# A two-layer transformer block on one core: the dense stream is written in even portions, with the next tokens' norm and gates moved

## The chip, the core and the metric

The kernel runs on one core of a Trainium2 chip. Its time is the device time in microseconds (us) of one execution; the median of three runs is compared. The engines are TensorE (PE; PEld is its weight load), VectorE (DVE), ScalarE (ACT), GpSimd (POOL) and SyncE (SP), which here only issues DMAs.

## The reference

The input is 4 sequences of 1024 tokens with 256 channels, float32. Two layers follow each other, each an attention part and a feed-forward part with adaptive layer norms (a norm, then a scale and a shift for each sequence, and a gate on the way back to the residual). Only the second layer is touched here:

```python
h = _layernorm(x) * (1 + ca) + sa
x = x + ga * _L1_attn_ref(h, ...)
h = _layernorm(x) * (1 + cb) + sb
x = x + gb * _L1_ffn_ref(h, ...)

def _L1_attn_ref(X, ...):                     # for each pair of tokens i, j of a sequence
    q, k = X @ Wq.T, X @ Wk.T                 # 64 channels
    e = relu(signed_sqrt(q[:, :, None, :] + k[:, None, :, :]))
    scores = e @ Wphi
    ex = exp(scores - max(scores))
    part1, Ew = ex @ Vy, einsum('bij,bija->bia', ex, e)
    return (part1 + Ew @ We_w.T + We_b * denom) / denom

def _L1_ffn_ref(x, ...):                      # 256 -> 1024 -> 1024 -> 1024 -> 256
    h = silu(x @ w1.T * s1) * (x @ w2.T * s2)
    h = gelu(h @ h1.T * sh1)
    h = gelu(h @ h2.T * sh2)
    return h @ w3.T * s3
```

## The kernel before

Up to about 1110 us the first layer runs. Then `pair_attention` does the second layer's attention and, woven into it, three other things.

**The attention loop.** The 4096 queries are taken in 128 blocks of 32. A block has 8 *turns*. In a turn VectorE weighs two tiles of 128 x 1024 (`weigh`, L1478: a product with a sum), and pairs for blocks ahead are made (`begin`, `make`): GpSimd or ScalarE or VectorE adds the query and clamps (L1402, L1407, L1427, L1416), ScalarE takes the square root (L1428), TensorE forms the scores (L1432). A ring of 14 tiles lets the making run ahead of the weighing. At turn p == 5 the scores' maximum is taken (`top`, L1442), at p == 6 the exponential (`exps`, L1451). ScalarE's tables for square root and exponential are changed there and back in each block (ACT_TABLE_LOAD). After every fourth block a task, `finish`, puts 128 tokens' attention together.

**The dense stream.** The feed-forward part is done for groups of 256 tokens, 16 groups in all. A group is put in the queue `stream` when `finish` has done its second 128 tokens, so every 8 blocks. It is a generator, `dense(j)`: `head` loads the residual and norms it; `gate` forms the first product, w1 (four pieces, L1263, evicted at L1255); silu; the second product, w2 (`up`, L1263, evicted with the product at L1298); two hidden layers of 1024 x 1024 (L1333, evicted at L1317), each followed by gelu; the output product (L1354), the gate (L1364) and the residual's sum (L1365). Two tiles, `wide[0]` and `wide[1]`, hold all that lies between. Weights come in tiles of 512 KB in a pool of four (`weights`, L1047), on SP's queue.

Ahead of the groups the stream has `first_rest` (the rest of the first layer) and, for each further sequence, `prepare` (its keys, queries and values; it uses `wide` too).

**The order.** All is written in one fixed order on the host; each engine then follows its own instructions in order. After the weighing of a turn `work(room)` advances first the tasks and then the stream:

```python
ROOM = (4, 6, 6, 6, 6, 4, 3, 6)      # units of TensorE's work in the turns of a block
...
got = next(of[0], self_done)         # a number: units written; None: wait for the next turn
```

An eviction is written `LATE = 2` turns after its products (`later`, `tick`). silu and gelu are not written at once: `between` keeps them, and `switch` writes them right behind the exponential, at p == 6, with a table load of their own. The stream waits for that (`while waiting: yield`): this is a *stop at ScalarE*. A group has three: silu, gelu, gelu. If another group is queued behind the current one (`follower`), its head and half of its gates are written behind the second hidden layer's products.

Of the kernel before, what the change touches and what calls it, by code (L numbers as in the profile page):

```python
# [7 lines left out]
F32 = mybir.dt.float32  # L8
AF = mybir.ActivationFunctionType
ALU = mybir.AluOpType  # L10
# [4 lines left out]
P = 128  # L15
B, T, C = 4, 1024, 256
# [10 lines left out]
FB = 256  # L27
# [3 lines left out]
RING = 14  # L31
PREP = 12
ROOM = (4, 6, 6, 6, 6, 4, 3, 6)
LATE = 2
ADDS = ('ap', 'pp', 'pp', 'dp', 'pp', 'ap', 'dp', 'ap')
FIRST_ON_SCALAR = 6
# [798 lines left out]
def pair_attention(tc, a, link, out, cols_of, seen, ident):  # L835
# [10 lines left out]
    nc = tc.nc  # L846
# [3 lines left out]
    with tc.tile_pool(name="at_k", bufs=1) as pk, tc.tile_pool(name="at_w", bufs=1) as wp, tc.tile_pool(  # L850
# [28 lines left out]
        same = wp.tile([P, P], F32, tag="same", name="same")  # L879
        part = wp.tile([P, 4], F32, tag="part", name="part")  # L880
        pick = wp.tile([P, 2, 2, P], F32, tag="pick", name="pick")
        ewt, ews = [], []
        for i in range(2):
            t = wp.tile([P, 4, P], F32, tag=f"ewt{i}", name=f"ewt{i}")
            nc.gpsimd.memset(t, 0.0)
            ewt.append(t)
            t = wp.tile([P, 4, 64], F32, tag=f"ew{i}", name=f"ew{i}")
            nc.gpsimd.memset(t, 0.0)
            ews.append(t)
# [153 lines left out]
        def weights(j, i, n=3):  # L1043
            for k in range(j * ALL + i, min(j * ALL + i + n, B * T // FB * ALL)):
                if k not in held:
                    held[k] = pfw.tile([P, DFF], F32, tag="fw", name="fw")
                    nc.sync.dma_start(held[k], a["ffw"][k % ALL * P : (k % ALL + 1) * P, :])  # L1047
            return held[j * ALL + i]

        def used(j, i):  # L1050
            held.pop(j * ALL + i)
# [5 lines left out]
        def bank(shape, name):  # L1057
            banks[0] -= 1
            return pg.tile(shape, F32, tag="g", name=name)

        def later(n, f):
            late.append([n, f])
# [178 lines left out]

        groups, heads, tokens = {}, {}, {}

        def gate(j, m):


            while not banks[0]:
                yield
            hT, to = wide[1][:, 0:2, :], (wide[1][:, 4 + m : 6 + m, :] if m < 4 else wide[0][:, m : m + 2, :])
            ps = bank([P, 2, FB], "ff_ps")  # L1250
            first_products(ps, weights(j, W1 + m // 4, 1 if m < 4 else 3), m, hT)
            if m % 4 == 2:
                used(j, W1 + m // 4)
            scale = fs[:, m : m + 2, 0:1].to_broadcast([P, 2, FB])
            later(LATE, lambda: nc.vector.tensor_tensor(to, ps, scale, ALU.mult))  # L1255
            yield 4

        def first_products(ps, w, m, hT):
            w = w.rearrange("p (k n) -> p k n", k=2)
            for h in range(2):  # L1260
                o = (m + h) % 4 * P
                for k in range(2):
                    nc.tensor.matmul(ps[:, h, :], w[:, k, o : o + P], hT[:, k, :], start=k == 0, stop=k == 1)  # L1263

        def head(j):

            heads[j] = tokens[j] = p2.tile([P, 2, C], F32, tag="res", name="res")
            nc.sync.dma_start(tokens[j], dst[j].rearrange("(t p) c -> p t c", p=P))
            yield
            yield  # L1270
            yield from normed(tokens[j], 2, j * FB // T, 3, wide[1][:, 0:2, :])
            for m in (0, 2):
                yield from gate(j, m)

        def follower():

            return groups.get(stream[1]) if len(stream) > 1 else None

        def dense(j):

            b = j * FB // T
            one, two = wide
            hT, gate_row = two[:, 0:2, :], rows[b]
            if j not in heads:
                yield from head(j)
            for m in (4, 6):
                yield from gate(j, m)
            while late:
                yield
            between(two[:, 4:8, :], AF.Silu)  # L1290
            between(one[:, 4:8, :], AF.Silu)
            while waiting:
                yield

            def up(ps, m):
                for h in range(2):
                    g = two[:, 4 + m + h, :] if m < 4 else one[:, m + h, :]
                    nc.vector.scalar_tensor_tensor(  # L1298
                        one[:, m + h, :], ps[:, h, :], fs[:, m + h, 1:2], g, ALU.mult, ALU.mult
                    )  # L1300

            for m in range(0, 8, 2):
                while not banks[0]:
                    yield
                ps = bank([P, 2, FB], "ff_ps")
                first_products(ps, weights(j, W2 + m // 4), m, hT)
                if m % 4 == 2:
                    used(j, W2 + m // 4)
                later(LATE, lambda ps=ps, m=m: up(ps, m))
                yield 4  # L1310
            while late:
                yield
            following = None
            for li, base, of, to in ((2, H1, one, two), (3, H2, two, one)):

                def hidden(ps, m):
                    nc.vector.tensor_tensor(  # L1317
                        to[:, m : m + 2, :], ps, fs[:, m : m + 2, li : li + 1].to_broadcast([P, 2, FB]), ALU.mult
                    )

                if li == 3 and follower() is not None:
                    following = head(follower())
                    next(following)
                for m in range(0, 8, 2):
                    if m == 4 and following is not None:
                        next(following)
                    while not banks[0]:
                        yield
                    ps = bank([P, 2, FB], "ff_ps")
                    for h in range(2):  # L1330
                        w = weights(j, base + m + h)
                        for k in range(8):
                            nc.tensor.matmul(  # L1333
                                ps[:, h, :], w[:, k * P : (k + 1) * P], of[:, k, :], start=k == 0, stop=k == 7
                            )
                            if k % 2 and (h == 0 or k < 7):
                                yield 2
                        used(j, base + m + h)
                    later(LATE, lambda ps=ps, m=m: hidden(ps, m))
                    yield 2  # L1340
                while late:
                    yield
                between(to, AF.Gelu)
                if following is not None:
                    yield from following
                while waiting:
                    yield
            while not banks[0]:
                yield
            ps = bank([P, 2, C], "out_ps")  # L1350
            w = [weights(j, W3 + i).rearrange("p (k n) -> p k n", k=4) for i in range(2)]
            for t in range(2):
                for k in range(8):
                    nc.tensor.matmul(  # L1354
                        ps[:, t, :], one[:, k, t * P : (t + 1) * P], w[k // 4][:, k % 4, :], start=k == 0, stop=k == 7
                    )
                    if k % 2 and (t == 0 or k < 7):
                        yield 2
            used(j, W3), used(j, W3 + 1)

            def last():
                fin, res = two[:, 2:4, :], tokens.pop(j)
                heads.pop(j)
                nc.vector.tensor_tensor(fin, ps, gate_row[:, 1:2, :].to_broadcast([P, 2, C]), ALU.mult)  # L1364
                nc.gpsimd.tensor_add(res, res, fin)  # L1365
                nc.sync.dma_start(out[j * FB : (j + 1) * FB, :].rearrange("(t p) c -> p t c", p=P), res)

            later(LATE, last)
            yield 2


# [2 lines left out]
        def between(t, func):  # L1374
            waiting.append(lambda: nc.scalar.activation(t, t, func))  # L1375
# [106 lines left out]
        def finish(n, ew, exT):  # L1482
# [8 lines left out]
                nc.tensor.transpose(ps[:, m, :], ew[:, m, :], ident)  # L1491
            yield
            yield
            z = ewt[i % 2]
            for u in range(2):
                for s in range(2):
                    r = 64 * u + 32 * s
# [68 lines left out]
        def work(room):  # L1566


            tick()
            turns[0] += 1  # L1570
            if issues and turns[0] % 2:
                issues.pop(0)()
            for of in (tasks, stream):
                while of and room > 0:
                    got = next(of[0], self_done)
                    if got is self_done:
                        of.pop(0)
                    elif got is None:
                        break
                    else:  # L1580
                        room -= got

        def begin():
            nonlocal begun
# [29 lines left out]
        for n in range(N):  # L1614
# [26 lines left out]
            if n % 4 == 3:  # L1641
                tasks.append(finish(n, ew, exT))
        while tasks or stream:
            work(16)
            switch()
        while late:
# [100 lines left out]
```

## Time and profile before

| | |
|---|---|
| median of 3 runs | 4834.72 us (4834.62 to 4846.67) |
| the profiled execution | 4844.85 us |
| its span (first to last instruction) | 4843.1 us |
| mean granted TensorE clock | 0.915 |
| attention blocks 0 to 127 | 1112.1 to 4694.5 us |
| after the last weigh | 148.6 us |
| w1/w2 products, L1263 | 1024 records, 411 ns each |
| hidden products, L1333 | 4096 records, 393 ns each |
| score products, L1432 | 16384 records, 411 ns each |
| square roots, L1428 | 1024, 1908 ns each |
| weighing, L1478 | 2048, 1213 ns each |

A float32 product of 256 columns shows as two records of TensorE. Records overlap, so their mean is longer than what one adds to the busy time. In windows each engine has its busy time and, in brackets, its instructions; behind the engines stand the granted clock of TensorE as a share of full speed, the share of DMA time and the GB/s. In the waits, a line has who waited, for whom, the time in all, how often, and the longest.

### The profile page before, as it was taken

To read this page: it belongs to the slowest core of one execution; us is meant where nothing else is said; L and a number is where in the kernel's file an instruction comes from. 1 tells how busy PE (TensorE), PEld (TensorE's weight loads), DVE (VectorE), ACT (ScalarE), POOL (GpSimd) and SP (SyncE) were. 2 spreads that over 40 slices of the span, in tenths; PEclk is the share of its full clock that TensorE was granted. 3 is DMA by queue.
4 is the path that set the end of the run, shared out by engine and by line. 5 is a ranking of instruction groups with operands and counts; after the bars stand their busy time and mean duration, and the time that the engine had idled before them with its cause. 6 is when DMAs were issued, how large, how long until landed. Compare 5 with 4: busy or idle time off the path is not lost. (4 is left out here: it accounts for less than half of the span.)

```text
span 4843.1 us, 76620 instructions
## 1 busy us (share of the span) xinstructions
PE 4253.5 (88%) x28714; PEld 2423.4 (50%) x28714; DVE 3881.2 (80%) x6834; ACT 3316.7 (68%) x3183; POOL 3573.9 (74%) x2942
## 2 busy tenths in 40 slices
PE   6899999986888889899897889898889899998888
PEld 1233333433335446555564556555446555555567
DVE  5899999767898888778877878878788878878771
ACT  2333233227888898778878878888788888878851
POOL 3544444337899898889888888888898888888840
PEclk8799999987889889999998999999899999999999
DMA  4344333441112123322222332222223322222223
GB/s 137 91 120 118 107 112 108 128 140 34 33 63 68 63 73 102 105 93 81 79 86 56 109 108 83 85 79 81 66 82 105 106 86 83 77 77 75 78 86 116
DMA packets 256965, 433.16 MB, mean 89 GB/s; under 512 B 71897, under 2 KB 142737, under 8 KB 256337
## 3 DMA queue, kind: packets, MB, share of 16 engines
q1 hardware_dynamic: 253520, 425.76, 28.3%
q8 instruction: 226, 3.70, 0.3%
q10 hardware_dynamic: 2880, 1.98, 0.1%
q14 instruction: 147, 1.20, 0.1%
q0 software_dynamic: 192, 0.52, 0.0%
HBM read 403.99 MB, written 40.93 MB: 92 GB/s over the span
## 5 line engine op out<-in xcount | busy, mean ns | idle before, releaser
L1478 DVE CUSTOM_DVE_ANT_0 s<-s,xb 128x1024 f32<-128x1024 f32 x2048 | 2393.1, 1213 | 63.9 <-PE xb L1458 47.1
L1428 ACT ACTIVATE s<-s 128x2048 f32<-128x2048 f32 x1024 | 1928.6, 1908 | 174.1 <-POOL s L1407 104.6
L1402 POOL TENSOR_SCALAR s<-kB,qt 128x1024 f32<-128x1024 f32 x1397 | 1600.0, 1151 | 281.8 <-DVE ew L1478 108.4
L1407 POOL TENSOR_SCALAR s<-s 128x1024 f32<-128x1024 f32 x1016 | 1421.4, 1399 | 89.1
L1432 PE MATMUL sc<-s,wsel 128*32 128x256 f32 x16384 | 1169.6, 411 | 332.8 <-ACT s L1428 331.6
L1333 PE MATMUL ff_ps<-wide,fw 128*128 128x256 f32 x4096 | 999.1, 393 | 25.1 <-ACT wide L1375 23.7
L1432 PEld LDWEIGHTS sc<-s,wsel 128*32 128x32 f32 x16384 | 456.7, 114 | 903.2 <-ACT s L1428 500.4
L1333 PEld LDWEIGHTS ff_ps<-wide,fw 128*128 128x128 f32 x4096 | 762.8, 193 | 231.3 <-issue 102.5
L741 POOL TENSOR_TENSOR kv<-vb,out_k 128x512 f32<-128x512 f32 x256 | 324.0, 1274 | 244.0 <-DVE state L809 167.4
L1427 ACT ACTIVATE s<-kB,qt 128x1024 f32<-128x1024 f32 x387 | 439.9, 1137 | 18.6 <-DMA kB<-kd 18.1
L616 PE MATMUL e_ps<-wd,hid 128*128 128x512 f32 x896 | 417.8, 613 | 7.0 <-DVE acc L599 4.5
L1458 PE MATMUL xb<-ex,pick 64*128 64x256 f32 x2048 | 320.8, 436 | 46.2 <-ACT ex L1451 46.0
L809 DVE TENSOR_TENSOR_SCAN state<-dec,carry,kv 128x512 f32<-128x512 f32 x256 | 326.2, 1274 | 23.4 <-ACT dec L796 17.5
L616 PEld LDWEIGHTS e_ps<-wd,hid 128*128 128x128 f32 x896 | 170.9, 196 | 233.1 <-issue 219.2
L1416 DVE TENSOR_SCALAR s<-kB,qt 128x1024 f32<-128x1024 f32 x264 | 285.9, 1085 | 0.0
L1263 PE MATMUL ff_ps<-wide,fw 128*128 128x256 f32 x1024 | 268.0, 411 | 17.7 <-DMA fw<-in_ffw_dram 17.0
L1458 PEld LDWEIGHTS xb<-ex,pick 64*128 64x128 f32 x2048 | 193.2, 204 | 180.2 <-ACT ex L1451 80.0
L1317 DVE TENSOR_TENSOR wide<-ff_ps,ffn_s 128x512 f32<-128x512 f32 x128 | 88.0, 687 | 212.2 <-PE ff_ps L1333 212.2
L1442 DVE TENSOR_REDUCE sc<-sc 128x1 f32<-128x256 f32 x128 | 55.1, 431 | 249.0 <-PE sc L1432 248.4
L801 ACT COPY carry<-state 128x1 f32<-128x1 f32 x255 | 47.9, 188 | 295.6 <-DVE state L809 295.3
L1263 PEld LDWEIGHTS ff_ps<-wide,fw 128*128 128x128 f32 x1024 | 200.2, 204 | 79.7 <-issue 35.9
L1451 ACT ACTIVATE ex<-sc,neg 128x256 f32<-128x256 f32 x128 | 60.7, 474 | 254.0 <-DVE neg L1449 252.6
(254 smaller groups left out, 4155.1 us busy)
## 6 DMA issues: line engine op xcount, KB each, us to landing
fw<-in_ffw_dram SPq DMA_DIRECT2D x361, 512.0 KB
vb<-vd SPq DMA_DIRECT2D x1024, 64.0 KB
lent<-vd SPq DMA_DIRECT2D x64, 514.0 KB
wd<-in_w_down_dram SPq DMA_DIRECT2D x28, 1024.0 KB
kB<-kd SPq DMA_DIRECT2D x32, 512.0 KB
lent<-in_We_dram SPq DMA_DIRECT2D x32, 512.0 KB
kd<-nd SPq DMA_DIRECT2D x24, 512.0 KB
vd<-out_v SPq DMA_DIRECT2D x8, 512.0 KB
```

The lines of the kernel that those rows point to most:

```text
L616: nc.tensor.matmul(ps, hid[:, k, t * P : (t + 1) * P], wd[:, k, :], start=k == 0, stop=k == HID // P - 1)
L741: nc.gpsimd.tensor_mul(kv, vb[:, g % 2, :], ready[u]["k"][:, n // HN, :])
L809: nc.vector.tensor_tensor_scan(s[:, 1 : U + 1], dec, kv, c, ALU.mult, ALU.add)
L1263: nc.tensor.matmul(ps[:, h, :], w[:, k, o : o + P], hT[:, k, :], start=k == 0, stop=k == 1)
L1333: nc.tensor.matmul(ps[:, h, :], w[:, k * P : (k + 1) * P], of[:, k, :], start=k == 0, stop=k == 7)
L1402: nc.gpsimd.tensor_scalar(self.s[p][:, h, :], kB[self.b][i % 8], 1.0, self.query(i), ALU.mult, ALU.add)
L1407: nc.gpsimd.tensor_scalar(both, both, FLT_MAX, 0.0, ALU.min, ALU.max)
L1427: nc.scalar.activation(t[:, h, :], kB[self.b][i % 8], AF.Relu, bias=self.query(i))
L1428: nc.scalar.activation(t, t, AF.Sqrt, bias=EPS_RHO)
L1432: nc.tensor.matmul(self.sc[32 * j : 32 * j + 32, 0:256], wsel[:, g, 16 * (1 - s) : 16 * (1 - s) + 32], t[:, h, 256 * j : 256 * (j + 1)], s ...
L1458: nc.tensor.matmul(xb[:, 256 * j : 256 * (j + 1)], pick[q, j % 2, s, :], self.ex[q, :], start=True, stop=True)
L1478: nc.vector.tensor_tensor_reduce(t[:, h, :], t[:, h, :], self.xb[s], 1.0, 0.0, ALU.mult, ALU.add, ew[:, self.n % 4, col : col + 1])
```

## The change

- The stream's units are paced. `even(units, most, less)` spreads a stage's units over the turns up to a stop at ScalarE: it takes the first stop at which the rate is not over `most` (4.2; 3.3 where the next tokens' gates are in it; 5.0 where more than two groups are queued, where something else than groups is queued, or in the last 12 blocks). `work` keeps a credit that grows by the rate each turn, and the stream goes on only while it is above 0.
- The next tokens' head (load, norm) becomes a list of its own, `side`, which `work` advances ahead of the stream; it runs beside the second hidden layer. It writes to a tile of its own, `hT`, in place of a part of `wide[1]`.
- The next tokens' gates, all four pieces, are written behind the second hidden layer's products and kept in `wide[1]` as a whole; silu is then one activation of 128 x 2048 and not two of 128 x 1024. The gelu and the silu are asked for when the last piece of each is evicted.
- The output's eviction and sum go in two halves, through a tile of the norm. `ewt` is one tile, not two. Fewer weights are called ahead of the gates and behind the output.
- After the last block the credit is set to 16 in each turn, so nothing is paced there but by the room.

```diff
--- before.py
+++ after.py
@@ -31,6 +31,7 @@
 RING = 14
 PREP = 12
 ROOM = (4, 6, 6, 6, 6, 4, 3, 6)
+EVEN, HALF, HURRY = 4.2, 3.3, 5.0
 LATE = 2
 ADDS = ('ap', 'pp', 'pp', 'dp', 'pp', 'ap', 'dp', 'ap')
 FIRST_ON_SCALAR = 6
@@ -879,11 +880,10 @@
         same = wp.tile([P, P], F32, tag="same", name="same")
         part = wp.tile([P, 4], F32, tag="part", name="part")
         pick = wp.tile([P, 2, 2, P], F32, tag="pick", name="pick")
-        ewt, ews = [], []
+        ewt, ews = wp.tile([P, 4, P], F32, tag="ewt", name="ewt"), []
+        nc.gpsimd.memset(ewt, 0.0)
+        hT = wp.tile([P, 2, FB], F32, tag="hT", name="hT")
         for i in range(2):
-            t = wp.tile([P, 4, P], F32, tag=f"ewt{i}", name=f"ewt{i}")
-            nc.gpsimd.memset(t, 0.0)
-            ewt.append(t)
             t = wp.tile([P, 4, 64], F32, tag=f"ew{i}", name=f"ew{i}")
             nc.gpsimd.memset(t, 0.0)
             ews.append(t)
@@ -1241,21 +1241,26 @@
 
         groups, heads, tokens = {}, {}, {}
 
-        def gate(j, m):
-
-
-            while not banks[0]:
-                yield
-            hT, to = wide[1][:, 0:2, :], (wide[1][:, 4 + m : 6 + m, :] if m < 4 else wide[0][:, m : m + 2, :])
-            ps = bank([P, 2, FB], "ff_ps")
-            first_products(ps, weights(j, W1 + m // 4, 1 if m < 4 else 3), m, hT)
-            if m % 4 == 2:
-                used(j, W1 + m // 4)
-            scale = fs[:, m : m + 2, 0:1].to_broadcast([P, 2, FB])
-            later(LATE, lambda: nc.vector.tensor_tensor(to, ps, scale, ALU.mult))
-            yield 4
-
-        def first_products(ps, w, m, hT):
+        def gates(j, n):
+
+            for m in range(0, 8, 2):
+                while not banks[0]:
+                    yield
+                ps = bank([P, 2, FB], "ff_ps")
+                first_products(ps, weights(j, W1 + m // 4, min(n, n + 1 - m // 4)), m)
+                if m % 4 == 2:
+                    used(j, W1 + m // 4)
+
+                def gated(ps=ps, m=m):
+                    scale = fs[:, m : m + 2, 0:1].to_broadcast([P, 2, FB])
+                    nc.vector.tensor_tensor(wide[1][:, m : m + 2, :], ps, scale, ALU.mult)
+                    if m == 6:
+                        between(wide[1], AF.Silu)
+
+                later(LATE, gated)
+                yield 4
+
+        def first_products(ps, w, m):
             w = w.rearrange("p (k n) -> p k n", k=2)
             for h in range(2):
                 o = (m + h) % 4 * P
@@ -1264,66 +1269,79 @@
 
         def head(j):
 
-            heads[j] = tokens[j] = p2.tile([P, 2, C], F32, tag="res", name="res")
+            tokens[j] = p2.tile([P, 2, C], F32, tag="res", name="res")
             nc.sync.dma_start(tokens[j], dst[j].rearrange("(t p) c -> p t c", p=P))
             yield
             yield
-            yield from normed(tokens[j], 2, j * FB // T, 3, wide[1][:, 0:2, :])
-            for m in (0, 2):
-                yield from gate(j, m)
+            yield from normed(tokens[j], 2, j * FB // T, 3, hT)
 
         def follower():
 
             return groups.get(stream[1]) if len(stream) > 1 else None
+
+        def even(units, most=EVEN, less=2):
+
+            t = turns[0]
+            end = t + 1 + (6 - t) % 8
+            if sum(g in groups for g in stream) > 2 or any(g not in groups for g in stream) or t > 8 * (N - 12):
+                most = HURRY
+            while units > most * (end - t - less):
+                end += 8
+            rate[0] = units / (end - t - less)
+            credit[0] = rate[0]
+
+        rate, credit, side = [0.0], [0.0], []
 
         def dense(j):
 
             b = j * FB // T
             one, two = wide
-            hT, gate_row = two[:, 0:2, :], rows[b]
+            gate_row = rows[b]
             if j not in heads:
+                heads[j] = True
                 yield from head(j)
-            for m in (4, 6):
-                yield from gate(j, m)
-            while late:
-                yield
-            between(two[:, 4:8, :], AF.Silu)
-            between(one[:, 4:8, :], AF.Silu)
-            while waiting:
+                even(16)
+                yield from gates(j, 3)
+                rate[0] = 0.0
+            while late or waiting:
                 yield
 
             def up(ps, m):
                 for h in range(2):
-                    g = two[:, 4 + m + h, :] if m < 4 else one[:, m + h, :]
                     nc.vector.scalar_tensor_tensor(
-                        one[:, m + h, :], ps[:, h, :], fs[:, m + h, 1:2], g, ALU.mult, ALU.mult
+                        one[:, m + h, :], ps[:, h, :], fs[:, m + h, 1:2], two[:, m + h, :], ALU.mult, ALU.mult
                     )
 
+            rate[0] = EVEN
             for m in range(0, 8, 2):
                 while not banks[0]:
                     yield
                 ps = bank([P, 2, FB], "ff_ps")
-                first_products(ps, weights(j, W2 + m // 4), m, hT)
+                first_products(ps, weights(j, W2 + m // 4), m)
                 if m % 4 == 2:
                     used(j, W2 + m // 4)
                 later(LATE, lambda ps=ps, m=m: up(ps, m))
                 yield 4
+            rate[0] = 0.0
             while late:
                 yield
-            following = None
+            follow = None
             for li, base, of, to in ((2, H1, one, two), (3, H2, two, one)):
 
                 def hidden(ps, m):
                     nc.vector.tensor_tensor(
                         to[:, m : m + 2, :], ps, fs[:, m : m + 2, li : li + 1].to_broadcast([P, 2, FB]), ALU.mult
                     )
-
-                if li == 3 and follower() is not None:
-                    following = head(follower())
-                    next(following)
+                    if m == 6:
+                        between(to, AF.Gelu)
+
+                if li == 3:
+                    follow = follower()
+                if follow is not None:
+                    heads[follow] = True
+                    side.append(head(follow))
+                even(*((64, EVEN) if follow is None else (80, HALF, 4)))
                 for m in range(0, 8, 2):
-                    if m == 4 and following is not None:
-                        next(following)
                     while not banks[0]:
                         yield
                     ps = bank([P, 2, FB], "ff_ps")
@@ -1338,17 +1356,18 @@
                         used(j, base + m + h)
                     later(LATE, lambda ps=ps, m=m: hidden(ps, m))
                     yield 2
-                while late:
-                    yield
-                between(to, AF.Gelu)
-                if following is not None:
-                    yield from following
-                while waiting:
+                if follow is not None:
+                    while side:
+                        yield
+                    yield from gates(follow, 1)
+                rate[0] = 0.0
+                while late or waiting:
                     yield
             while not banks[0]:
                 yield
+            rate[0] = EVEN
             ps = bank([P, 2, C], "out_ps")
-            w = [weights(j, W3 + i).rearrange("p (k n) -> p k n", k=4) for i in range(2)]
+            w = [weights(j, W3 + i, 2 - i).rearrange("p (k n) -> p k n", k=4) for i in range(2)]
             for t in range(2):
                 for k in range(8):
                     nc.tensor.matmul(
@@ -1359,13 +1378,16 @@
             used(j, W3), used(j, W3 + 1)
 
             def last():
-                fin, res = two[:, 2:4, :], tokens.pop(j)
+                res = tokens.pop(j)
                 heads.pop(j)
-                nc.vector.tensor_tensor(fin, ps, gate_row[:, 1:2, :].to_broadcast([P, 2, C]), ALU.mult)
-                nc.gpsimd.tensor_add(res, res, fin)
+                for t in range(2):
+                    fin = p2.tile([P, C], F32, tag="ln_xn", name="fin")
+                    nc.vector.tensor_tensor(fin, ps[:, t, :], gate_row[:, 1, :], ALU.mult)
+                    nc.gpsimd.tensor_add(res[:, t, :], res[:, t, :], fin)
                 nc.sync.dma_start(out[j * FB : (j + 1) * FB, :].rearrange("(t p) c -> p t c", p=P), res)
 
             later(LATE, last)
+            rate[0] = 0.0
             yield 2
 
 
@@ -1491,7 +1513,7 @@
                 nc.tensor.transpose(ps[:, m, :], ew[:, m, :], ident)
             yield
             yield
-            z = ewt[i % 2]
+            z = ewt
             for u in range(2):
                 for s in range(2):
                     r = 64 * u + 32 * s
@@ -1568,10 +1590,11 @@
 
             tick()
             turns[0] += 1
+            credit[0] = min(credit[0] + rate[0], 8.0)
             if issues and turns[0] % 2:
                 issues.pop(0)()
-            for of in (tasks, stream):
-                while of and room > 0:
+            for of in (tasks, side, stream):
+                while of and room > 0 and (of is not stream or not rate[0] or credit[0] > 0):
                     got = next(of[0], self_done)
                     if got is self_done:
                         of.pop(0)
@@ -1579,6 +1602,8 @@
                         break
                     else:
                         room -= got
+                        if of is stream:
+                            credit[0] -= got
 
         def begin():
             nonlocal begun
@@ -1641,6 +1666,7 @@
             if n % 4 == 3:
                 tasks.append(finish(n, ew, exT))
         while tasks or stream:
+            credit[0] = 16.0
             work(16)
             switch()
         while late:
```

## The prediction

> **What bounds the kernel now.** I read the page first, then the windows, the waits of the attention stretch, and the timeline of the end.
>
> ```profile
> PE 4253.5 (88%) x28714; PEld 2423.4 (50%) x28714; DVE 3881.2 (80%) x6834; ACT 3316.7 (68%) x3183; POOL 3573.9 (74%) x2942
> ```
>
> No engine is full over the span. The change touches only what follows first_rest: 116 blocks of attention (blocks 12 to 127, 1459.7 to 4694.5 us) and the end. A block is 8 turns; I cut blocks at their first weigh on VectorE (L1478). Windows, in the order PE, PEld, DVE, ACT, POOL, then clock:
>
> ```profile
> 2235.60:2261.70 26.10, 26.10 (x217) 17.29 (x218) 21.85 (x39) 23.21 (x20) 24.56 (x21) 1.00 0.33 103
> 2288.60:2321.80 33.20, 32.27 (x233) 21.71 (x234) 22.87 (x41) 25.54 (x19) 25.42 (x20) 0.93 0.25 80
> 2378.50:2402.90 24.40, 21.68 (x189) 13.12 (x189) 23.63 (x44) 20.50 (x16) 21.99 (x19) 0.93 0.35 115
> 2129.50:2288.60 159.10, 146.42 (x1216) 92.42 (x1215) 138.43 (x252) 138.43 (x106) 144.99 (x119) 0.95 0.27 87
> 1459.70:4694.50 3234.80, 2868.64 (x23284) 1795.47 (x23285) 2654.06 (x4825) 2682.56 (x2034) 2792.33 (x2275) 0.93 0.26 84
> 4694.50:4843.10 148.60, 127.46 (x552) 108.50 (x550) 18.78 (x37) 16.16 (x16) 4.35 (x5) 0.93 0.37 123
> ```
>
> Lines 1 to 3 are blocks 40, 42 and 45. A block with many dense products is held by TensorE (42: 32.27 of 33.20 us busy), one with few by VectorE (45: 23.63 of 24.40). Line 5: over all 116 blocks four engines are within 215 us of each other, so whoever is overfull in one block is idle in the next. The waits of that stretch say so:
>
> ```profile
> PE sc L1432 <- ACT s L1428: 271.3, 169, 8.4
> ACT ex L1451 <- DVE neg L1449: 242.3, 57, 7.6
> DVE sc L1442 <- PE sc L1432: 212.2, 67, 8.6
> DVE wide L1317 <- PE ff_ps L1333: 120.3, 42, 5.4
> ```
>
> It is a ring: late products hold the maxima on VectorE, these hold the exponential on ScalarE, and the square roots queued behind that hold TensorE.
>
> **Counting the order.** The order of writing is fixed on the host, so the dense products per turn can be stepped through from the rules alone. One unit is one 256-column product, two records in the trace. A group has 32 first + 128 hidden + 16 output = 176 units. Stepped so, the order of before gives 42 units for block 42's hidden layer, and the trace has 85 records; it leaves 256 units for the end, and the trace has 64 + 390 + 64 = 518 records there. The steps can be trusted.
>
> Stepping the order of after:
> - Steady group: up takes 5 turns, the first hidden layer 64/19 = 3.37 a turn, the second with the next gates 80/28 = 2.86 over 32 turns, the output 5. A group takes 64 turns. A new one comes every 64 turns: nothing is caught up.
> - Before, a group with another queued behind it takes about 54 turns, so each prepare (25 turns) is made good.
> - HURRY hardly helps at the end, since a layer is rounded up to the next ScalarE stop, 8 turns apart. At turn 961 the stops end at 967, 975, 983; 64/(14-2) = 5.33 is over 5.0, so the layer gets 22 turns at 3.2.
> - So group 12 ends at turn 1019 (before: 923), and the blocks end with group 13 before its first hidden layer and 14 and 15 untouched: 496 units for the end instead of 256.
>
> **Cost at the end.** The engine at work there is TensorE alone:
>
> ```profile
> 4750.20 16.14 PE L1263 MATMUL ff_ps<-wide,fw 128*128 128x256 f32 x64 [0.71 <-ACT wide L947]
> 4766.18 27.79 PE L1333 MATMUL ff_ps<-wide,fw 128*128 128x256 f32 x128
> 4798.03 29.58 PE L1333 MATMUL ff_ps<-wide,fw 128*128 128x256 f32 x128 [4.06 <-ACT wide L1375]
> 4830.40 7.17 PE L1354 MATMUL out_ps<-fw,wide 128*128 128x256 f32 x32 [2.79 <-ACT wide L1375]
> ```
>
> A hidden unit takes (27.79 + 29.58)/128 = 0.45 us, a first one 16.14/32 = 0.50, an output one 7.17/16 = 0.45. The extra 192 hidden, 32 first and 16 output units cost 86 + 16 + 7 = 109. Pauses: before 15.6 us (2.3, 2.7, 3.0, 0.7, 4.1, 2.8). After there are eight stops of some 2.7 us, 21 us, and no exposed norm: +6. Sum **+115 us**.
>
> **Gain in the blocks.** In the 116 blocks 2320 units are left of 2560. Blocks with 32 or more units fall from 40 to 8. Outside the twelve blocks with prepare in them, before's block times by units written are: 25.98 us (up to 12 units, 22 blocks), 26.80 (13 to 21, 18), 27.35 (22 to 31, 24), 29.28 (32 and more, 40). After has 12, 21, 60 and 8 such blocks, 22.6 units on average, and 15 with prepare. Those I put at the old times, 12 x 29.42 + 3 x 25.98 = 431 us.
> - Upper bound, only the counts change: (12 x 25.98 + 21 x 26.80 + 60 x 27.35 + 8 x 29.28) / 101 = 27.23 us a block; 2750 + 431 = 3181, gain 54.
> - Lower bound: GpSimd's 2792.33/116 = 24.1 us is the fullest engine once TensorE has given 109 us to the end (2760 left). One us more for the ring: 25.0; gain 279.
> - Nearest row: blocks 36 to 41 (fourth window line) have 12 to 34 units, 22.3 on average, two or three stops and a norm among them: 159.10/6 = 26.5. Block 36 still pays for block 35's 42 units (34.35 us); without it the five take 25.95. I take **26.2**, between the two: 101 x 26.2 + 431 = 3077, gain **158 us**.
>
> **Smaller edits.**
> - Stops: the second layer's last eviction falls at turn 22 + 2 of 32, just before the stop at 24, and the gates go to the one at 32. So there are still three stops in most groups; 46 in all by my steps, 48 before. Even a merged stop saves no load, for silu and gelu change the table between them:
>
> ```profile
> 4760.26 1.06 ACT L1375 ACTIVATE wide<-wide 128x1024 f32<-128x1024 f32 x1 [2.46 <-DVE wide L1255]
> 4794.78 1.28 ACT L1375 ACT_TABLE_LOAD   x1 [33.46 <-DVE wide L1317]
> 4796.07 1.91 ACT L1375 ACTIVATE wide<-wide 128x2048 f32<-128x2048 f32 x1
> ```
>
>   Gain 0; bounds 0 and 16 x 1.28 = 20 us. The Trainium skill, page "ScalarE: Activation LUTs", section "Table sets: the hidden batching unit", says to batch calls by table set and lists gelu in a set of its own; this speaks against the third part of the change. The page puts a switch at about 2.66 us with a drain, which the rows above do not show (load 1.28, next start 0.01 after it); by its figure 16 saved switches would be 43 us.
> - Norm beside the layer: 16 heads as before, but the residual load now has two turns of notice. It is queued on SP behind weight loads that wait for free tiles; VectorE's statistics wait for it, and behind them the weighs. Seven heads of before had the same notice, and that wait is 3.8 us in all. The square root behind the statistics cost ScalarE 54.7 us in 14 heads, 3.9 each, and stays. Cost 0; bounds -55 and +55, a wait gone or doubled.
> - Weight loads fall from 361 to 352 (16 x 22), each 0.33 us of SP's issue; TensorE waited 17.0 us for weights in the stretch, three times, beside the reload of kB. Taken as staying; bounds -17 and +17.
> - One ewt: its next writer comes four blocks (some 105 us) later. The output in two halves: two of about 0.48 for one of 0.69 on VectorE, two of 0.78 for one of 1.28 on GpSimd, 9 us in all over 16 groups, off the path. Taken as 0.
>
> **Sum.** -158 + 115 = -43 us. The profiled execution took 4844.85 us (span 4843.1), 10 above the median of 4834.72; -43 on the median is **4792 us**.
>
> **Rivals.**
> - *The end decides* (slower). Place: the tail after the last weigh. Price 115, fixed by the counts. It wins when the 101 blocks average above 26.62 us ((3234.8 - 115 - 431)/101). For: the bins give 27.23, hence 4834.7 + 115 - 54 = 4896. Against: those bins hold bursts of 6 units a turn; after writes mostly 4 or fewer. Chance 0.37.
> - *Even out* (26.48 to 26.76 a block): within 0.3%, 14.5 us, about what a measurement of this kernel can tell from no change. The six-block row, 26.5, gives 4823. Chance 0.13.
> - *The ring closes up*: 25.0 a block, 4834.7 - 279 + 115 = 4671. For: TensorE drops below GpSimd. Against: no stretch of six blocks of before went under 26.4. Chance 0.08.
> - *It does not do what it says*: true of the stops, by my count; its price is the 0 above.
>
> **Numbers.** The forecast case, 25.4 to 26.48 a block, gets 0.42; with the closed ring, faster 0.50; same 0.13; slower 0.37. The range runs from 25.3 (4702, put at 4705) to the bins' end, 4895.
>
> **What would show it.** The stretch after the last weigh near 264 us with some 990 dense records; 46 stops at ScalarE; 101 blocks near 26.2 and few above 30; the maxima's wait on TensorE (212.2) more than halved. I am wrong if that wait stays, if the end is shorter than 230 us, or if new waits for the residual load or weights appear on VectorE or TensorE.

## The result, and the profile after

The changed kernel takes 4885.91 us (median of 5 runs, 4881.85 to 4895.47), the kernel before 4843.61 us in the same count of runs. The ratio is 1.0098, 95% interval 1.0082 to 1.0114: **slower by 1%, some 42 us**. The forecast was 43 us faster; the time lies inside the range, on the side of the rival.

The page's first part, of the changed kernel, beside the line shown before: no engine is busier by more than 6.5 us, and TensorE is busy 10 us less.

```profile
PE 4243.5 (87%) x28714; PEld 2401.5 (49%) x28714; DVE 3882.4 (79%) x6850; ACT 3319.7 (68%) x3169; POOL 3580.4 (73%) x2957
```

So the 41 us more of span (4883.7 after 4843.1) are in the main waits. The windows of the changed kernel: the stretch of blocks 12 to 127, the end, then blocks 69, 70 and 71.

```profile
1454.30:4613.80 3159.50, 2757.28 (x22806) 1680.71 (x22806) 2641.01 (x4805) 2670.85 (x2009) 2795.26 (x2285) 0.93 0.24 79
4613.80:4883.60 269.80, 234.48 (x1028) 201.27 (x1028) 36.34 (x73) 30.72 (x27) 7.12 (x11) 0.95 0.38 126
2994.40:3028.60 34.20, 28.17 (x216) 18.41 (x216) 23.34 (x47) 23.72 (x17) 27.34 (x24) 0.90 0.28 97
3028.60:3051.50 22.90, 22.90 (x200) 14.06 (x199) 22.81 (x44) 20.38 (x15) 18.50 (x16) 1.00 0.22 70
3051.50:3076.10 24.60, 24.04 (x205) 14.89 (x204) 22.62 (x38) 20.95 (x16) 23.19 (x19) 1.00 0.20 66
```

The stretch is 75 us shorter than before (3234.8), the end 121 us longer (148.6); the work ahead of block 12 differs by 5 us. An evenly filled block goes very well: block 70 takes 22.90 us with TensorE busy throughout and VectorE for 22.81. But block 69, with hardly more instructions, takes 34.20, and all five engines idle in it. Such a block comes once a group, where one group hands over to the next: blocks 33, 41, 61, 69, 77, 96, 103, 111 and 119 take 33.9 to 42.4 us.

The waits of the stretch, in the columns of before (who for whom, us, times, longest):

```profile
PE sc L1454 <- ACT s L1450: 274.8, 178, 7.3
DVE sc L1464 <- PE sc L1454: 179.8, 76, 10.0
ACT ex L1473 <- DVE neg L1471: 171.4, 47, 10.2
DVE wide L1332 <- PE ff_ps L1351: 70.8, 30, 4.9
PE ff_ps L1268 <- DMA fw<-in_ffw_dram: 58.8, 13, 8.1
PEld ff_ps L1268 <- DMA fw<-in_ffw_dram: 17.2, 3, 6.9
```

Most of the old waits shrank (the hidden layers' evictions 120.3 to 70.8, the exponential 242.3 to 171.4, the maxima only 212.2 to 179.8); TensorE's wait for square roots did not (271.3 to 274.8). New is that w1/w2 products wait for weights: 58.8 us in the stretch, after 17.0, and 72.2 us over the run. The 17.2 us of the weight load (PEld) are the same stalls, seen a second time (blocks 111, 119 and 127), so they are not added. Block 69 shows how such a stall comes about. First SP's timeline, then TensorE's, then the engines behind it:

```profile
3006.03 0.33 SPq L1576 DMA_DIRECT2D x<-xr  x1
3013.76 0.39 SPq L1387 DMA_DIRECT2D out_dram<-res  x1
3014.20 1.90 SPq L1047 DMA_DIRECT2D fw<-in_ffw_dram  x4
```

```profile
3011.69 1.93 PE L1454 MATMUL sc<-s,wsel 128*32 128x256 f32 x32
3018.79 3.75 PE L1268 MATMUL ff_ps<-hT,fw 128*128 128x256 f32 x8 [5.16 <-DMA fw<-in_ffw_dram]
3023.56 0.39 PE L1467 MATMUL sc<-quarters,same 128*128 128x4 f32 x2
```

```profile
3012.31 1.42 POOL L1386 TENSOR_TENSOR res<-res,fin 128x256 f32<-128x256 f32 x2 [2.01 <-DVE fin L1385]
3023.98 0.16 DVE L1471 TENSOR_REDUCE neg<-sc 128x1 f32<-128x4 f32 x1 [6.33 <-PE sc L1467]
3024.18 0.47 ACT L1473 ACTIVATE ex<-sc,neg 128x256 f32<-128x256 f32 x1 [10.16 <-DVE neg L1471]
```

The output's store (L1387) stands on SP until the group's last sum on GpSimd (L1386) is there, at 3013.76. The w2 tiles are called at up, which is written behind that store, so SP issues them only at 3014.20, and the first w2 product starts at 3018.79. Behind it in TensorE's order stands the small product of the block's maximum (L1467, 3023.56); VectorE waits 6.33 us for that, ScalarE's exponential 10.16 for VectorE, and the square roots stand behind the exponential.

The kernel before had a handover too, in its block 38, which took 23.1 us. SP, then TensorE:

```profile
2170.98 14.79 SPq L1047 DMA_DIRECT2D fw<-in_ffw_dram  x4
2192.18 0.40 SPq L1366 DMA_DIRECT2D out_dram<-res  x1
2207.34 2.33 PE L1263 MATMUL ff_ps<-wide,fw 128*128 128x256 f32 x8
```

By the order of the calls, the last two of these four loads are the w2 tiles, so they go ahead of the store. And half the gates and a stop at ScalarE lay between the output and up: the first w2 product starts 15 us behind the store, not 5, and does not wait for weights. In three of the nine such handovers of before the w2 tiles do go behind the store (at 3282.28, for one), and up still comes late enough for them.

The end has two such stalls as well, one for each group that hands over there:

```profile
4704.21 9.45 PE L1268 MATMUL ff_ps<-hT,fw 128*128 128x256 f32 x32 [6.81 <-DMA fw<-in_ffw_dram]
4795.93 9.67 PE L1268 MATMUL ff_ps<-hT,fw 128*128 128x256 f32 x32 [6.63 <-DMA fw<-in_ffw_dram]
```

### The profile page after: what moved, and what is told of

Same layout as the page of the kernel before. It is cut to its first block, busy times and chain, and to the rows that moved or that the text cites. A ratio compares the mean times of both kernels' runs of the same rounds, so it can differ in the third digit from the quotient of the medians.

```text
span 4883.7 us, 76703 instructions
## 1 busy us (share of the span) xinstructions
PE 4243.5 (87%) x28714; PEld 2401.5 (49%) x28714; DVE 3882.4 (79%) x6850; ACT 3319.7 (68%) x3169; POOL 3580.4 (73%) x2957
## 5 line engine op out<-in xcount | busy, mean ns | idle before, releaser
L1500 DVE CUSTOM_DVE_ANT_0 s<-s,xb 128x1024 f32<-128x1024 f32 x2048 | 2390.5, 1211 | 58.8 <-PE xb L1480 50.9
L1351 PE MATMUL ff_ps<-wide,fw 128*128 128x256 f32 x4096 | 1012.3, 392 | 34.4 <-ACT wide L1397 30.1
L1351 PEld LDWEIGHTS ff_ps<-wide,fw 128*128 128x128 f32 x4096 | 749.7, 192 | 256.0 <-issue 122.2
L1268 PE MATMUL ff_ps<-hT,fw 128*128 128x256 f32 x1024 | 278.8, 424 | 78.8 <-DMA fw<-in_ffw_dram 72.2
L1480 PE MATMUL xb<-ex,pick 64*128 64x256 f32 x2048 | 311.0, 425 | 41.2 <-ACT ex L1473 40.9
L1268 PEld LDWEIGHTS ff_ps<-hT,fw 128*128 128x128 f32 x1024 | 206.7, 211 | 140.7 <-issue 74.7
L812 DVE TENSOR_TENSOR pr<-state,rec 128x512 f32<-128x512 f32 x256 | 176.0, 687 | 37.6 <-ACT state L808 9.6
```

The lines of the kernel that those rows point to most:

```text
L1351: nc.tensor.matmul(ps[:, h, :], w[:, k * P : (k + 1) * P], of[:, k, :], start=k == 0, stop=k == 7)
L1480: nc.tensor.matmul(xb[:, 256 * j : 256 * (j + 1)], pick[q, j % 2, s, :], self.ex[q, :], start=True, stop=True)
L1500: nc.vector.tensor_tensor_reduce(t[:, h, :], t[:, h, :], self.xb[s], 1.0, 0.0, ALU.mult, ALU.add, ew[:, self.n % 4, col : col + 1])
```

## The experiments

Theory A: the loss is this late call of weights. Theory B: the end decides, as in the rival; the wait hides behind others. Spans are of the profiled executions; ratios are to the kernel before, on the same chip. The runs were on three chips, where the kernel before took 4841.3 to 4842.2 us.

**The w2 tiles called earlier.**

```diff
+            if follow is not None:
+                weights(follow, W2, 2)     # stands behind W3's own call, at the start of the output product
```

> After, with one call more: the follower's two w2 tiles are asked for at the start of the output product, ahead of the output's store on SP. Theory A (queue): the loss of the change is at the handover of groups. There SP issues the w2 tiles behind the store, which waits for the group's last sum; TensorE waits 5.16 us for them in block 69, and VectorE 6.33, ScalarE 10.16 behind it; blocks 33, 41, 61, 69, 77, 96, 103, 111, 119 and 127 take 28 to 42 us, the others some 25. A expects the wait of w1/w2 products for weights (72.2 us) to fall under 25, those ten blocks to fall by 8 us or more, the stretch of 116 blocks from 3160 to 3050 to 3090 us, the end unchanged near 270, and 4775 to 4815 us in all, faster than before. Theory B (the end decides): the 240 units moved to the end cost 115 to 121 us and the even blocks give back only about that much less 40; the wait for weights hides behind TensorE's other waits, so 4865 to 4890 us.

Measured 4811.17 us, ratio 0.9935 (0.992 to 0.995): 75 us less than the change as it was, and faster than before. The windows of this kernel, stretch, end and block 69:

```profile
1450.60:4550.70 3100.10, 2746.66 (x22806) 1674.98 (x22806) 2645.03 (x4805) 2671.55 (x2009) 2794.41 (x2285) 0.94 0.25 81
4550.70:4801.70 251.00, 228.43 (x1028) 197.21 (x1028) 36.36 (x73) 30.72 (x27) 7.12 (x11) 0.97 0.40 136
2973.60:3001.60 28.00, 27.52 (x224) 18.15 (x227) 24.42 (x46) 24.04 (x17) 24.44 (x22) 1.00 0.33 114
```

With the same instructions the stretch loses 59 us and the end 19. Block 69 goes from 34.20 to 28.00, with TensorE at 1.00 of its clock and not 0.90. The wait of TensorE for weights over the whole run, after and then here:

```profile
PE ff_ps L1268 <- DMA fw<-in_ffw_dram: 72.2, 15, 8.1
PE ff_ps L1268 <- DMA fw<-in_ffw_dram: 12.4, 6, 2.8
```

The time and this wait are as theory A expected. Its parts are off: eight of the nine blocks named above fall by 5 us or more, but only one by the 8 expected; the stretch stays 10 us above the expected bound; the end was to stay, and loses its two stalls. Theory A holds for 75 us.

**The store behind up.** The call stays late; only the store moves.

```diff
-                nc.sync.dma_start(out[...], res)
+                stores.append(lambda: nc.sync.dma_start(out[...], res))
...
+            while stores:          # behind the products of up
+                stores.pop(0)()
```

> After, with one edit: the output's store is written behind the next group's up products and no longer ahead of them; the w2 tiles are asked for at up, as in after. It tells apart two readings of the late weights. A1 (the store blocks SP): SP is then free to issue the w2 tiles as soon as their places in the pool are free, so the wait goes as it did with the earlier call: 4800 to 4830 us, TensorE's wait for weights in the w1/w2 products under 30 us. A2 (the call itself is too late, whatever is ahead of it): at most 15 us better than after, 4870 to 4890 us, the wait above 55 us. Theory B (the wait does not matter): 4875 to 4890 us whatever becomes of it, which the run with the earlier call already speaks against.

Measured 4810.03 us, ratio 0.9939 (0.9919 to 0.9959), the same as with the earlier call; the w1/w2 products wait 8.2 us for weights over the run. SP's timeline at the same handover:

```profile
2994.09 0.33 SPq L1578 DMA_DIRECT2D x<-xr  x1
2994.83 5.44 SPq L1047 DMA_DIRECT2D fw<-in_ffw_dram  x4
3001.91 0.40 SPq L1389 DMA_DIRECT2D out_dram<-res  x1
```

The weights now go 0.74 us behind the attention's store, 7 us ahead of the output's. Reading A1 is shown: the call was not too late by itself, it stood behind a store that waits for a result.

**No pacing**, with the late and with the early call. Rates of 100 leave the stream to the turns' room.

```diff
-EVEN, HALF, HURRY = 4.2, 3.3, 5.0
+EVEN, HALF, HURRY = 100.0, 100.0, 100.0
```

> After with the three rates at 100, so the stream is held by the turns' room alone, as in before; the norm beside, the gates behind and the weights' calls stay. By the order 256 units are left for the end, as in before, and 37 blocks have 32 units or more (before 40). Theory A: the end goes back to some 150 us, the bursts come back, the waits for weights stay: 4870 to 4930 us. Theory B: with the end short again the loss is gone: 4820 to 4850 us.

> The unpaced form with the two w2 tiles asked for ahead of the output's store. Theory A: what is left of the change beside pacing and the late weights is about nothing, so near before, 4820 to 4860 us, and 40 to 100 us under the unpaced form without the call. Theory B: equal to the unpaced form without the call, within 15 us.

Measured 4877.94 us with the late call, ratio 1.0075 (1.006 to 1.009), and 4814.32 with the early one, 0.9943 (0.9928 to 0.9958). The windows of the first, then of the second:

```profile
1460.00:4732.50 3272.50, 2868.74 (x23295) 1799.39 (x23293) 2645.24 (x4840) 2679.14 (x2020) 2794.86 (x2289) 0.93 0.25 82
4732.50:4881.80 149.30, 126.55 (x541) 107.39 (x541) 18.05 (x38) 14.16 (x14) 4.63 (x7) 0.93 0.32 108
```

```profile
1450.00:4659.00 3209.00, 2845.16 (x23295) 1785.47 (x23293) 2649.10 (x4840) 2680.85 (x2020) 2797.05 (x2289) 0.93 0.26 84
4659.00:4811.00 152.00, 129.57 (x541) 109.64 (x541) 18.11 (x39) 14.16 (x14) 4.62 (x7) 0.92 0.31 107
```

Four forms make a square:

| stretch + end, us | w2 behind the store | w2 ahead of it |
|---|---|---|
| paced | 3159.5 + 269.9 | 3100.1 + 251.1 |
| not paced | 3272.4 + 149.3 | 3208.9 + 152.7 |

Pacing takes 113 or 109 us from the stretch and gives the end 121 or 98: nothing that stays (by the medians 8 us slower with the late call, 3 faster with the early one). The early call takes 78 or 60 us with and without pacing. Theory B is wrong on the cause: with the end short again, the unpaced form is as slow as the change. The unpaced form with the early call is still 28 us under the kernel before, so what else the change does, beside pacing, is worth something.

**The norm in line.** The unpaced form with the early call, its head written behind the layer's products.

```diff
-                    side.append(head(follow))
...
-                    while side:
-                        yield
+                    yield from head(follow)
```

> The unpaced form with the w2 tiles ahead, and the next tokens' load and norm written behind the second layer's products, ahead of the gates, not beside the layer. It asks what the norm beside is worth. If the square root and the statistics of the norm stop the engines as much in either place: within 15 us of 4814. If the norm beside the layer hides it: slower by 3 to 5 us for each of 12 groups, 4850 to 4875 us.

Measured 4859.04 us, ratio 1.0042 (1.0027 to 1.0056): 45 us slower than with the norm beside. But not through waits in the blocks: its stretch is shorter (3115.1 us) and its end longer (283.5, with 1056 dense records for 512). The time falls in the range expected of a norm hidden beside the layer, but by another way: in line, the head's turns are added to each group's way, and more of the stream is left for the end. The norm beside is worth turns; what it saves in stalls this run does not show.

**A shorter end with some pacing.** Three ways, each with the early call.

```diff
-            rate[0] = units / (end - t - less)                     # e4
+            rate[0] = EVEN
...
-EVEN, HALF, HURRY = 4.2, 3.3, 5.0                                  # e6
+EVEN, HALF, HURRY = 4.2, 4.2, 7.0
...
-EVEN, HALF, HURRY = 4.2, 3.3, 5.0                                  # e5
+EVEN, HALF, HURRY = 4.2, 3.3, 7.0
-            if sum(g in groups for g in stream) > 2 or ...
+            if sum(g in groups for g in stream) > 1 or ...
```

> The w2 tiles asked for ahead, and a flat rate of 4.2 units a turn in every stage in place of a rate stretched to the next stop at ScalarE. By the order 320 units are left for the end (after 496, before 256), 24 blocks have 32 units or more (after 8, before 40), and 37 stops are made (46, 48). Theory A: the end near 180 us, the blocks a little slower than in the stretched form: 4740 to 4790 us, the fastest of the four. Theory B: the end is the larger term, so 4790 to 4830 us through the shorter end alone.

> The w2 tiles ahead; 4.2 for the layer with gates too, hurry at 7.0 for three groups queued. By the order 386 units are left for the end, 18 blocks have 32 units or more, and 40 stops are made, the gelu and the silu mostly in one stop. If stops merged are worth something, it is under the form with the earlier call (4811) by more than the end gains: the end some 45 us shorter, the blocks some 25 slower, so 4790 us without a worth of merged stops, 4770 or less with one of 3 us each.

> The w2 tiles ahead; the hurried rate at 7.0 and not 5.0, and already where two groups are queued and not three. By the order 300 units are left for the end (496 in after), 18 blocks have 32 units or more (8). It asks whether even portions pay once the end is not lengthened. If units cost about 0.5 us at the end and evenness is worth about 1 us a block, as the stretch of the paced and the unpaced form say (3100 and 3209 us): the end near 175 us, the stretch near 3150, so 4765 to 4795 us. If what the end gains is lost again in the blocks: 4800 to 4815 us.

| | time, ratio | stretch + end, us | dense records at the end |
|---|---|---|---|
| e4, flat rate | 4801.38, 0.9917 (0.9901 to 0.9934) | 3189.8 + 154.3 | 512 |
| e6, gates' layer at 4.2, hurry at 7.0 | 4820.03, 0.9958 (0.9948 to 0.9969) | 3147.8 + 210.5 | 779 |
| e5, hurry early | 4788.02, 0.9892 (0.9871 to 0.9914) | 3181.9 + 155.1 | 584 |

The early hurry is the best version found, 1.1% faster than before. Its two windows:

```profile
1453.70:4635.60 3181.90, 2833.67 (x23218) 1757.10 (x23218) 2652.67 (x4837) 2681.37 (x2018) 2801.12 (x2289) 0.94 0.26 83
4635.60:4790.70 155.10, 138.31 (x618) 118.65 (x616) 20.87 (x43) 18.63 (x17) 4.64 (x7) 0.97 0.38 129
```

e5 keeps 27 us of the stretch against the unpaced form and gives 2 to the end. Its time is in the expected range partly by luck: the stretch came out 32 us above what was expected, the end 20 below. In e6 the stops fall to the expected 40, but the loads stay at 47, and it is 9 us slower than the early call alone, so merged stops bring nothing that shows. e4 lies where theory B expected it, above theory A's range; its end has 256 units, not the 320 I had stepped, and why was not followed up.

**Two edges of the best version**: no rate where a second group is queued (7.0 to 100), and the output evicted four turns behind its products.

```diff
-            later(LATE, last)
+            later(LATE + 2, last)
```

> The early hurry with its rate at 100 and not 7.0, so that the stream is paced only where no second group is queued. By the order 256 units are left for the end (300 with 7.0) and 26 blocks have 32 units or more (18). If evenness still pays at this edge, it is slower than the early hurry: 4790 to 4815 us. If the last 44 units at the end weigh more: 4765 to 4785 us.

> The early hurry (4788 us) with the output's eviction written four turns behind its products and not two. In the early hurry VectorE waits 75.7 us in 14 groups for the output products, 5.4 us each, with the weighs queued behind it. If that wait is a loss of its own: 40 us or more less, 4735 to 4755 us. If TensorE is late there in any case and the weighs would wait for it at the next maximum: within 15 us of 4788.

Measured 4799.69 us, 0.9915 (0.9894 to 0.9936), and 4795.01 us, 0.9911 (0.9893 to 0.9928): neither is better. The first has 3196.0 + 148.5 us. In the second VectorE's wait for the output products, 75.7 us, is gone from the list, but its wait for the scores goes from 188.5 to 213.6; the stretch is 13 us shorter and the end 19 us longer (173.9, with 656 dense records for 584). As a whole, taking the wait away gained nothing.

## Why the prediction was wrong

- **The step that failed** is "Weight loads fall from 361 to 352 ... Taken as staying; bounds -17 and +17". The number of loads was right (352), but I looked at how many there are and how long one takes, not at what stands ahead of each on SP. Before, the gates behind the output called both w2 tiles, mostly ahead of the store and with a stop still to come before up; after, w2 is called at up, behind a store that waits for GpSimd, and is needed at once. Measured: TensorE's wait for weights over the run from 17.0 to 72.2 us, and 75 us of time by the medians (4885.9 to 4811.2 with the earlier call; in the profiled executions 59 in the stretch and 19 at the end). That is larger than the outcome's 42 us, and it alone turns the sign. I named a new wait for weights as what would prove me wrong, and priced it at 17 us at most.
- **The sum of pacing**, -158 + 115 = -43, did not hold either. The runs that differ in pacing alone show -109 + 98 with the early call and -113 + 121 with the late one: 3 us gained, or 8 lost, by the medians. What put the early form 31 us under the kernel before is mostly what I took as 0: the unpaced form with the early call is 28 us under it already. The norm beside, worth 45 us in the run with the norm in line, is the one part of this that a run isolates.
- **Gain in the blocks**, 158 us, for pacing and fewer units together: measured 75 with the late weights and 135 without them (3234.8 to 3100.1). The row that I took 26.2 from held a handover, at 2192.18, but one with the w2 tiles ahead of the store. In the changed kernel blocks 62 to 67 take 22.9 to 29.1 us, 25.1 on average, under what I took; 68 and 69 (30.2 and 34.2) give it back. That the stretch, 3159.5 us, comes near the upper bound of 3181, where only the counts change, is chance. The sign that I named for the mechanism, the maxima's wait more than halved from 212.2, did not come: 179.8, and 148.1 with the early call. Nor did "few above 30": there are 21 blocks above 30 us, after 23.
- **Cost at the end**, +115 us: measured +121, with the 992 dense records that the steps of the order gave (496 units). The count held exactly. The price is right partly by luck: 13 us of it are the two stalls for weights, which were not in my sum, and with the early call it is +102.
- **Stops**: 46 by my steps, no load saved. The trace has 48 activations of 2048 in 46 stops, and 47 loads, against 64 activations and 46 loads before; a silu is now one activation, and nearly every activation still costs a load:

```profile
L1397 ACT ACTIVATE wide<-wide x48: 1909/1911/1916, 1480.2 to 4867.6; 128x2048 f32<-128x2048 f32 x48
L1397 ACT ACT_TABLE_LOAD  x47: 1283/1283/1283, 1478.9 to 4834.0; - x47
```

  The Trainium skill, page "ScalarE: Activation LUTs", section "Table sets: the hidden batching unit", says to batch calls by table set and not by function. The counts agree as far as they go: 46 stops took 47 loads, the 40 of e6 took 47 and the 37 of e4 took 46, so merging a gelu's stop with a silu's saved next to none.
- **The norm beside**, 0 with bounds of 55: ScalarE's wait for the statistics fell from 68.4 to 16.4 us, VectorE's for the residual rose from 4.3 to 15.8. A change in both directions inside the bounds; its larger worth, the turns it frees (45 us between the two unpaced forms), was not in my sum.
- **The rival** "the end decides" had the right side and nearly the right time (4896), for a wrong reason: blocks that only follow their counts. Its price, the end, is real and is paid back by pacing. (Against the rival of the closed ring I wrote that no six blocks of before went under 26.4 us; the last six, 122 to 127, take 25.9.)

## What to carry to other kernels

When a step is moved, look at each load it calls in the issuing queue's order: here a store that waited for a result held every load written behind it, and the 0.33 us that a load's issue takes said nothing about the wait. Pacing a stream trades time in the middle for work left at the end, so both must be read in the same unit; here they cancelled until the pace was let go wherever a second group was waiting. And a wait taken off a list is not a gain by itself: with the output's eviction written later 75.7 us of waiting went, and the time did not fall.

## What was not expected of the hardware

An even block can run at 22.90 us with TensorE and VectorE both busy all through (22.90 and 22.81 us) and a granted clock of 1.00, below the 24.1 us that GpSimd needs for a block on average. GpSimd is busy for 27.34 us in the stalled block 69 and for 18.50 in block 70, so the ring's tiles made in a stalled block are used up in the next ones. So a fast block beside a slow one says little; only sums over a group do.
